# A decoder layer's expert stage: routing of two batches traced beside the items, weights in twelve buffers, products for counts five steps behind the choice, three experts with a first small item

## The chip, the cores and the metric

The kernel runs on one core of a Trainium2 chip. A core has five engines with a queue of instructions each, and a queue is worked through in order: TensorE (PE; its weight loads are shown apart as PEld), VectorE (DVE), ScalarE (ACT), GpSimd (POOL) and SyncE (SP), which here only issues DMAs. The metric is the device time of one execution in microseconds (us). Three executions of the kernel before gave 679.78, 682.89 and 682.9 us, with a median of 682.89 us.

## What is computed

One decoder layer on x of shape (4, 512, 256), in float32, three sublayers with a LayerNorm after each residual sum:

```python
x = layernorm(x + mamba(x))                    # scan over 512 steps, 16 states
x = layernorm(x + mlstm(q=x, k=ctx, v=ctx))    # 4 heads, causal, gated
# mixture of experts: 2048 tokens, 8 experts, the best two for each token
logits = x @ gate_w
mult, sel = sparse_mixer_top2(logits)
h = silu(einsum('th,ehf->etf', x, w1)) * einsum('th,ehf->etf', x, w3)
out = einsum('etf,efh,te->th', h, w2, w)       # w: mult at the chosen experts
x = layernorm(x + out)
```

An expert's weights are w1 and w3 (256 x 1024 each) and w2 (1024 x 256), 1 MB each. The kernel multiplies only the tokens that chose an expert.

## The kernel before

The first sublayer takes the trace up to about 165 us and is not touched. The rest is `layers23`.

**Attention** (`attend_fast`) goes over eight pairs of batch and half of the heads. In iteration n it makes the scores of pair n and the values of pair n-1, in four parts `tb`; the sums of the pair before that are gathered at the start (`gathered`, `gather`). When both pairs of a batch are gathered, a generator `finish(b)` is put into `tails`: this is the batch's **routing tail**. It holds the head norm (`den`, `vr`), logits and the first choice (`route`), the residual rows `hv`, then `close`: the statistics of the second LayerNorm (`norm_stats`), the normed rows `x`, which SP stores to DRAM (`xd`, up to three copies, and `yd`), and the rest of `route`. In `route`, two choices per token give `hot`; five small matrix products of `hot` (line 1717, the products for counts) give each token's position in its expert's list; DVE makes one-hot tiles `olo` and `oval`; eight products of those (line 1754) make `by`, the list of tokens by slot; `tables` turns it into the int32 tables for the gathers; a softmax (`ex`, `wk`) gives the multipliers, which are transposed (line 1792) and stored to DRAM (`wd`). The generator stops at each `yield`; `step()` runs the next piece of the oldest tail. In the kernel before, every part `tb` calls `step()` twice, so that the tails of batches 0, 1 and 2 are traced between parts of attention. Each tail has two square roots and one exponential on ACT.

**Experts.** An item is one block (128 tokens of an expert; "small item") or two blocks (256). `work` takes a list of items in order: `turn` (gathered rows are transposed, line 1277, DVE copies them), `up` (products with w1 and w3, line 1292; ACT takes Silu, line 1297; DVE multiplies, line 1298; one piece for each `yield`), then `down` of the item before (products with w2, line 1316; ACT weighs, line 1336; POOL adds the rows into `yd` by an indirect DMA, line 1322). Rows are gathered by POOL, two items ahead (`fetch`, line 1248). `early` holds one small item of each of the first NEARLY experts, with tokens of batches 0 and 1 only; `mid` a two-block item of each expert above NEARLY, with tokens of the first three batches, and another of expert 7; `late` all that is left but one expert, and five items whose expert is known only at run time; that one expert, number NEARLY, is taken by `finale` as four small items. With NEARLY at 2 there are 12 two-block items and 13 small ones, 37 blocks.

**Weights.** `load_expert` issues three DMAs of 1 MB on SP (w1, w3, w2) into one of three sets of tiles in turn. Two sets are loaded ahead of attention. The third set lies where attention keeps `x1T` and `val`, and can be filled only after these are done with. When the first item of an expert has been traced, the load of the expert two further on is traced. A `w1` tile becomes free when the former expert's `up` has ended, a `w2` tile when its `down` has.

**Order.** What is traced first has priority, but a planner orders each engine's queue when the program is built: from its own estimates of times it takes the first traced instruction that it holds to be ready. `keep_in_program_order` ties an instruction behind the one traced just before it on the same engine. In the layout of the pools, `np_` has one buffer for each name, `rt` two, the PSUM pool `pu` of `up` three banks, and `pt` (transposes and sums of heads) two.

At the end of `layers23` the kernel before does this, where `tails` then holds batch 3's tail alone:

```python
*done, last = tails
weights, pending = xp.work(xp.early, weights, xp.mid)
for _ in last:
    pass
weights, pending = xp.work(xp.mid + xp.late, weights, [xp.final], overflow_at_item_1, pending)
return xp.finale(xp.final, weights[0], pending)
```

So batch 3's tail is traced as one piece between the early items and the middle ones.

Of the kernel before, what the change touches and what calls it, by code (L numbers as in the profile page):

```python
# [27 lines left out]
NEARLY = 2  # L28
# [15 lines left out]
def decoder_kernel(ctx: ExitStack, tc: tile.TileContext, t: dict, out: bass.AP):  # L44
# [14 lines left out]
    def norm_stats(sp, src, n, tag):  # L59

        st = sp.tile([P, n, 6], F32, tag=tag + "st", name=tag + "st")
        mv = sp.tile([P, n, 2], F32, tag=tag + "mv", name=tag + "mv")
        for i in range(n):
            nc.vector.bn_stats(out=st[:, i, :], in_=src[:, i, :])
            nc.vector.bn_aggr(out=mv[:, i, :], in_=st[:, i, :])
        sd = sp.tile([P, n], F32, tag=tag + "sd", name=tag + "sd")
        nc.scalar.activation(sd, mv[:, :, 1], AF.Sqrt, bias=eps5)
        rs = sp.tile([P, n], F32, tag=tag + "rs", name=tag + "rs")
        nc.vector.reciprocal(rs, sd)
        return mv, rs  # L70
# [931 lines left out]
    def attend_fast(ap, hrp, np_, pt, tri, onw, mix, part, gatew, close, rt, route):  # L1002
# [4 lines left out]
        with ExitStack() as hs:  # L1007
# [170 lines left out]
            for n in range(len(pairs) + 1):  # L1178
# [6 lines left out]
                for tb in range(NB):  # L1185
# [13 lines left out]
                    step()  # L1199
                    step()  # L1200
# [14 lines left out]
    def experts(o, fast):  # L1215
# [5 lines left out]
        def load_expert(e):  # L1221

            nonlocal loads
            ew = o.ring[loads % 3]
            loads += 1
            w1 = ew.tile([P, 2, FF], F32, tag="w1", name="w1")
            w3 = ew.tile([P, 2, FF], F32, tag="w3", name="w3")
            w2 = ew.tile([P, NF, D], F32, tag="w2", name="w2")
            for w, n in ((w1, "w1"), (w3, "w3"), (w2, "w2")):
                nc.sync.dma_start(  # L1230
                    out=w, in_=t[n][bass.ds(e, 1)].rearrange("o (k p) f -> p (o k) f", p=P)
                )
            return w1, w3, w2
# [50 lines left out]
        def up(xT_, G, w1, w3, ht):  # L1284

            N, U = G * P, TS // (G * P)
            for f in range(0, NF, U):
                ps = o.pup.tile([P, 2, U, N], F32, tag="pu", name="pu")
                for u in range(U):
                    for j, w in enumerate((w1, w3)):  # L1290
                        for k in range(2):
                            nc.tensor.matmul(  # L1292
                                ps[:, j, u, :], w[:, k, (f + u) * P : (f + u + 1) * P],
                                xT_[:, k, :N], start=(k == 0), stop=(k == 1),
                            )
# [18 lines left out]
        def product(ps, g, G, ht, w2):  # L1314
            for f in range(NF):
                nc.tensor.matmul(  # L1316
                    ps, ht[:, (f * G + g) * P : (f * G + g + 1) * P], w2[:, f, :],
                    start=(f == 0), stop=(f == NF - 1),
                )
# [19 lines left out]
        def work(visits, weights, ahead=(), between=None, pending=None):  # L1339
# [6 lines left out]
            for i, (n, v, cols) in enumerate(line):  # L1346
# [4 lines left out]
                for _ in up(xT_, G, w1, w3, ht):  # L1351
                    pass
# [199 lines left out]
    def layers23(fast):  # L1552
# [4 lines left out]
        with ExitStack() as rest:  # L1557
# [125 lines left out]
            def route(b, base):  # L1683
# [32 lines left out]
                for i in range(5):  # L1716
                    nc.tensor.matmul(
                        pc, one_b if i else tri_b, hot[:, 4 - i : 9 - i, :],
                        start=(i == 0), stop=(i == 4),
# [29 lines left out]
                for j in range(NK):  # L1749
# [4 lines left out]
                    nc.tensor.matmul(  # L1754
                        pk, olo[:, j, :], oval[:, j, :], start=(j == 0), stop=(j == NK - 1)
# [36 lines left out]
                nc.tensor.transpose(bank[:NK, 384:], wk, ident)  # L1792
# [7 lines left out]
            def close(b, hv, routing=None):  # L1800
# [5 lines left out]
                mv, rs = norm_stats(np_, hv, NB, "n2")  # L1806
                yield
                next(routing)
# [10 lines left out]
                for rows in (*xds[max(b - 1, 0) :], yd):  # L1819
                    nc.sync.dma_start(  # L1820
                        out=rows[b * S : (b + 1) * S, :].rearrange("(i p) d -> p i d", p=P), in_=xb
                    )
                yield
# [102 lines left out]
            if tails:  # L1926
                *done, last = tails
                for tail in done:
                    for _ in tail:
                        pass  # L1930
            else:
                last = iter(())
            weights, pending = xp.work(xp.early, weights, xp.mid)
            for _ in last:
# [3 lines left out]
                pending,  # L1938
# [121 lines left out]
```

## Time and profile before

| What | Value |
|---|---|
| Median of three executions | 682.89 us |
| Profiled execution, its own time | 681.57 us |
| Span of its trace | 679.7 us |
| TensorE busy in the span | 645.8 us (95%) |
| VectorE, ScalarE, GpSimd busy | 307.8, 241.1, 209.0 us |
| Moved by DMA | 92.89 MB, mean 137 GB/s |
| Granted TensorE clock, mean | 0.978 |
| Weight DMAs | 57 of 1 MB |

Each line of the page's groups, or of a timeline, gives the engine, the line of the kernel, the operation, the tile written and those read with their shapes, and how many instructions are merged; a bracket at the end is idle time of that engine just before, and what ended it. float32 products appear as two records each, so a small item has 64 records of line 1292 and 16 of line 1316. A clock of 0.50 means that TensorE was granted half of its speed.

### The profile page before, as it was taken

How to read it: one execution, taken by the hardware profiler on the slowest of the kernel's cores; microseconds unless marked ns; L12 is line 12 of the kernel's file. 1: busy time of each engine (PE TensorE's matmuls, PEld its weight loads, DVE VectorE, ACT ScalarE, POOL GpSimd, SP SyncE). 2: the span in 40 equal slices, each digit the busy share in tenths (PEclk: the TensorE clock that was granted, in tenths of full speed). 3: DMA queues.
4: the chain of work that ended last, by engine and by line, in shares of the span. 5: the costliest groups of instructions: out<-in, count | busy, mean ns of one | idle time of the engine just before them, and what ended most of it. 6: DMA issues, size and time to landing. Idle time of an engine off the chain costs nothing. (4 is left out here: it accounts for less than half of the span.)

```text
span 679.7 us, 9237 instructions
## 1 busy us (share of the span) xinstructions
PE 645.8 (95%) x3447; PEld 497.9 (73%) x3447; DVE 307.8 (45%) x799; ACT 241.1 (35%) x473; POOL 209.0 (31%) x244
## 2 busy tenths in 40 slices
PE   6999999999997987899999999999999999999994
PEld 2434577766353447788888888888888899999993
DVE  1969658797557899662222221111211121121641
ACT  3965472132775754541121221112111111111452
POOL 0033400000564572743423244322432323423202
PEclk9999999999997996999999999999999999999998
DMA  8300501004603066856755335644463524883531
GB/s 279 121 1 0 186 1 32 31 1 160 242 1 124 9 196 216 285 170 209 220 169 179 86 94 154 194 153 137 150 209 78 152 78 148 272 316 86 176 113 36
DMA packets 61671, 92.89 MB, mean 137 GB/s; under 512 B 8904, under 2 KB 48784, under 8 KB 61360
## 3 DMA queue, kind: packets, MB, share of 16 engines
q1 hardware_dynamic: 52432, 80.51, 34.7%
q0 software_dynamic: 8096, 9.60, 7.2%
q10 hardware_dynamic: 1088, 2.10, 0.9%
q8 instruction: 29, 0.48, 0.3%
q14 instruction: 26, 0.21, 0.1%
HBM read 78.78 MB, written 14.06 MB: 137 GB/s over the span
## 5 line engine op out<-in xcount | busy, mean ns | idle before, releaser
L1292 PE MATMUL pu<-xgT,w 128*128 128x128 f32 (+1 forms) x1600 | 266.3, 327 | 1.0 <-DVE ht L1298 0.9
L1292 PEld LDWEIGHTS pu<-xgT,w 128*128 128x128 f32 x1600 | 243.0, 193 | 22.7 <-ACT x L1391 1.1
L1298 DVE TENSOR_TENSOR ht<-pu,si 128x256 f32<-128x256 f32 x148 | 62.6, 424 | 229.5 <-ACT si L1297 229.2
L1316 PE MATMUL po<-w,ht 128*128 128x256 f32 x592 | 136.7, 381 | 0.0
L1297 ACT ACTIVATE si<-pu 128x256 f32<-128x256 f32 x148 | 56.8, 384 | 195.6 <-PE pu L1292 195.3
L1316 PEld LDWEIGHTS po<-w,ht 128*128 128x128 f32 x592 | 109.8, 191 | 14.6 <-ACT y L1336 0.6
L1322 POOL DMA_INDIRECT yd<-y,tab x33 | 53.3, 1614 | 143.3 <-ACT y L1336 125.7
L232 PE MATMUL xz<-xT,win 128*128 128x512 f32 x128 | 58.3, 616 | 6.3 <-DMA xT<-in_xT 5.8
L1248 POOL DMA_INDIRECT xg<-xd,tab x37 | 36.8, 993 | 82.7 <-PE pt L1277 59.5
L232 PEld LDWEIGHTS xz<-xT,win 128*128 128x128 f32 x128 | 24.9, 198 | 38.8 <-issue 30.4
L1336 ACT ACTIVATE y<-po,wg 128x256 f32<-128x256 f32 x33 | 15.6, 474 | 93.8 <-PE po L1316 93.8
L1038 POOL TENSOR_TENSOR ct<-ct,tri 128x128 f32<-128x128 f32 x64 | 32.7, 530 | 34.0 <-ACT ct L1037 33.4
L460 PE MATMUL fpy<-mt,xs 128*128 128x384 f32 (+3 forms) x128 | 36.8, 438 | 0.5 <-DVE fsz L464 0.5
L255 DVE SCALAR_TENSOR_TENSOR acc<-xp,convw,acc 128x1024 f32<-128x1024 f32 x24 | 29.3, 1286 | 14.2 <-ACT acc L250 14.2
L1037 ACT ACTIVATE ct<-pq,eT 128x512 f32<-128x512 f32 (+3 forms) x64 | 29.9, 524 | 15.3 <-PE pq L1026 15.2
L1307 POOL DMA_INDIRECT wg<-wd,tab x33 | 31.9, 967 | 9.9 <-issue 9.6
L1026 PE MATMUL pq<-x1T,ctxT 64*128 64x512 f32 (+3 forms) x128 | 33.0, 486 | 1.6 <-ACT ct L1037 1.2
L1281 DVE COPY xgT<-pt 128x512 f32<-128x512 f32 (+1 forms) x22 | 12.5, 569 | 41.4 <-PE pt L1277 41.4
L460 PEld LDWEIGHTS fpy<-mt,xs 128*128 128x128 f32 x128 | 22.1, 190 | 12.3 <-issue 6.2
L485 PE MATMUL fpo<-fwout,fsz 128*128 128x256 f32 x128 | 28.9, 382 | 0.1
L485 PEld LDWEIGHTS fpo<-fwout,fsz 128*128 128x128 f32 x128 | 23.8, 190 | 4.7 <-issue 0.8
L1026 PEld LDWEIGHTS pq<-x1T,ctxT 64*128 64x128 f32 x128 | 13.7, 188 | 17.5 <-issue 8.0
(260 smaller groups left out, 612.9 us busy)
## 6 DMA issues: line engine op xcount, KB each, us to landing
w<-in_w SPq DMA_DIRECT2D x57, 1024.0 KB
xd<-x SPq DMA_DIRECT2D x9, 512.0 KB
xT<-in_xT ACTq DMA_DIRECT2D x4, 512.0 KB
ctxT<-in_ctxT SPq DMA_DIRECT2D x1, 2048.0 KB
val<-in_ctx SPq DMA_DIRECT2D x4, 512.0 KB
fxr<-in_x SPq DMA_DIRECT2D x4, 512.0 KB
yd<-x SPq DMA_DIRECT2D x4, 512.0 KB
x<-yd SPq DMA_DIRECT2D x4, 512.0 KB
```

What stands on the lines that cost most here:

```text
L232: nc.tensor.matmul(ps, win[:, k, c * P : (c + 1) * P], xT[:, k, b * S : (b + 1) * S], start=(k == 0), stop=(k == 1),)
L460: nc.tensor.matmul(ps[:, j * P :], xs[j][:, c, :], mt[b][j], start=(j == 0), stop=(j == NB - 1),)
L485: nc.tensor.matmul(ps, sz[:, c, b * S + i * P : b * S + (i + 1) * P], wout[:, c, :], start=(c == 0), stop=(c == NC - 1),)
L1026: nc.tensor.matmul(pss[e][:, cols[-1]], ctxT[rows, p, s0 : s0 + P], x1T[rows, p, s0 : (b + 1) * S], start=True, stop=True,)
L1038: nc.gpsimd.tensor_tensor(ct[:, :P], ct[:, :P], tri, ALU.mult)
L1248: nc.gpsimd.indirect_dma_start(out=xg[:, g, :], out_offset=None, in_=xds[min(v, 2)][:, :], in_offset=bass.IndirectOffsetOnAxis(ap=tok[v][: ...
L1292: nc.tensor.matmul(ps[:, j, u, :], w[:, k, (f + u) * P : (f + u + 1) * P], xT_[:, k, :N], start=(k == 0), stop=(k == 1),)
L1297: nc.scalar.activation(si, ps[:, 0].rearrange("p u n -> p (u n)"), AF.Silu)
L1298: nc.vector.tensor_tensor(ht[:, f * N : (f + U) * N], ps[:, 1].rearrange("p u n -> p (u n)"), si, ALU.mult)
L1307: issue = nc.gpsimd.indirect_dma_start(out=wg, out_offset=None, in_=wds[min(v, 2)][:, :], in_offset=bass.IndirectOffsetOnAxis(ap=wat[v][:, ...
L1316: nc.tensor.matmul(ps, ht[:, (f * G + g) * P : (f * G + g + 1) * P], w2[:, f, :], start=(f == 0), stop=(f == NF - 1),)
L1322: return nc.gpsimd.indirect_dma_start(out=rows[:, :], out_offset=bass.IndirectOffsetOnAxis(ap=dest[v][:, c : c + 1], axis=0), in_=src, in_ ...
```

## The change

Five edits, in the order of the file.

1. NEARLY goes from 2 to 3. `early` has three small items (experts 0, 1, 2), `mid` four two-block items (experts 4 to 7) and expert 7's second; `finale` takes expert 3. There are 11 two-block items and 15 small ones, still 37 blocks and 19 loads of an expert.
2. In attention, `step()` is no longer called in the last two iterations (n = 7 and 8). Batch 2's tail is left in `tails`, beside batch 3's.
3. `work` takes a generator `beside` and draws from it once after each piece of `up`. The early items get batch 2's tail, two steps a draw; the middle items get batch 3's tail, two steps a draw.
4. A tail has three more steps between the choice and the products for counts. These, the products for the list, the transpose of the multipliers, and the `bn_stats` of the second LayerNorm are tied behind what is traced just before them.
5. Weights are loaded in twelve pieces of 256 KB, each in a tile of its own: four of w1, four of w3, four of w2. A piece of w1 or w3 has 256 columns, so that a row in DRAM is cut into runs of 1 KB instead of 4 KB. The products read the piece that they need.

```diff
--- before.py
+++ after.py
@@ -1,4 +1,5 @@
 from contextlib import ExitStack
+from itertools import chain, zip_longest
 from types import SimpleNamespace
 
 import numpy as np
@@ -25,7 +26,7 @@
 NE, FF = 8, 1024
 NTT = NT // P
 TS = 256
-NEARLY = 2
+NEARLY = 3
 NOV = 31
 NOV0 = 5
 HCLIP = 100.0
@@ -56,12 +57,14 @@
         nc.sync.dma_start(out=c, in_=src)
         return c
 
-    def norm_stats(sp, src, n, tag):
+    def norm_stats(sp, src, n, tag, keep=False):
 
         st = sp.tile([P, n, 6], F32, tag=tag + "st", name=tag + "st")
         mv = sp.tile([P, n, 2], F32, tag=tag + "mv", name=tag + "mv")
         for i in range(n):
-            nc.vector.bn_stats(out=st[:, i, :], in_=src[:, i, :])
+            bn = nc.vector.bn_stats(out=st[:, i, :], in_=src[:, i, :])
+            if keep:
+                tc.keep_in_program_order(bn)
             nc.vector.bn_aggr(out=mv[:, i, :], in_=st[:, i, :])
         sd = sp.tile([P, n], F32, tag=tag + "sd", name=tag + "sd")
         nc.scalar.activation(sd, mv[:, :, 1], AF.Sqrt, bias=eps5)
@@ -1196,8 +1199,9 @@
                         residual(n // NH)
                     if n:
                         values(*pairs[n - 1], tb, cts[tb], po)
-                    step()
-                    step()
+                    if n < len(pairs) - 1:
+                        step()
+                        step()
                 if n:
                     sums = (*pairs[n - 1], po, hraw, sq2)
                 cts = nxt
@@ -1223,12 +1227,26 @@
             nonlocal loads
             ew = o.ring[loads % 3]
             loads += 1
-            w1 = ew.tile([P, 2, FF], F32, tag="w1", name="w1")
-            w3 = ew.tile([P, 2, FF], F32, tag="w3", name="w3")
-            w2 = ew.tile([P, NF, D], F32, tag="w2", name="w2")
-            for w, n in ((w1, "w1"), (w3, "w3"), (w2, "w2")):
+            w1, w3 = (
+                [ew.tile([P, 2, 2 * P], F32, tag=f"{n}{q}", name=n) for q in range(NF // 2)]
+                for n in ("w1", "w3")
+            )
+            w2 = [ew.tile([P, 2, D], F32, tag=f"w2{q}", name="w2") for q in range(NF // 2)]
+
+            for q in range(NF // 2):
+                for w, n in ((w1, "w1"), (w3, "w3")):
+                    nc.sync.dma_start(
+                        out=w[q],
+                        in_=t[n][bass.ds(e, 1), :, 2 * P * q : 2 * P * (q + 1)].rearrange(
+                            "o (k p) f -> p (o k) f", p=P
+                        ),
+                    )
+            for q in range(NF // 2):
                 nc.sync.dma_start(
-                    out=w, in_=t[n][bass.ds(e, 1)].rearrange("o (k p) f -> p (o k) f", p=P)
+                    out=w2[q],
+                    in_=t["w2"][bass.ds(e, 1), 2 * P * q : 2 * P * (q + 1), :].rearrange(
+                        "o (k p) f -> p (o k) f", p=P
+                    ),
                 )
             return w1, w3, w2
 
@@ -1287,10 +1305,11 @@
             for f in range(0, NF, U):
                 ps = o.pup.tile([P, 2, U, N], F32, tag="pu", name="pu")
                 for u in range(U):
+                    cols = slice((f + u) % 2 * P, ((f + u) % 2 + 1) * P)
                     for j, w in enumerate((w1, w3)):
                         for k in range(2):
                             nc.tensor.matmul(
-                                ps[:, j, u, :], w[:, k, (f + u) * P : (f + u + 1) * P],
+                                ps[:, j, u, :], w[(f + u) // 2][:, k, cols],
                                 xT_[:, k, :N], start=(k == 0), stop=(k == 1),
                             )
                 si = o.sip.tile([P, U * N], F32, tag="si", name="si")
@@ -1314,7 +1333,7 @@
         def product(ps, g, G, ht, w2):
             for f in range(NF):
                 nc.tensor.matmul(
-                    ps, ht[:, (f * G + g) * P : (f * G + g + 1) * P], w2[:, f, :],
+                    ps, ht[:, (f * G + g) * P : (f * G + g + 1) * P], w2[f // 2][:, f % 2, :],
                     start=(f == 0), stop=(f == NF - 1),
                 )
 
@@ -1336,7 +1355,7 @@
                 nc.scalar.activation(y[:, g, :], ps[:, g, :], AF.Copy, scale=wg[:, g : g + 1])
                 scatter(yd, v, c, y[:, g, :], compute_op=ALU.add)
 
-        def work(visits, weights, ahead=(), between=None, pending=None):
+        def work(visits, weights, ahead=(), between=None, pending=None, beside=iter(())):
 
 
 
@@ -1349,7 +1368,7 @@
                 w1, w3, w2 = weights[n]
                 ht = inner(G)
                 for _ in up(xT_, G, w1, w3, ht):
-                    pass
+                    next(beside, None)
                 if i + 2 < len(line):
                     xgs.append(fetch(*line[i + 2][1:]))
                 if pending is not None:
@@ -1714,9 +1733,11 @@
                 yield
                 pc = bank[:, 32 : 32 + 5 * NE].rearrange("p (n e) -> p n e", e=NE)
                 for i in range(5):
-                    nc.tensor.matmul(
-                        pc, one_b if i else tri_b, hot[:, 4 - i : 9 - i, :],
-                        start=(i == 0), stop=(i == 4),
+                    tc.keep_in_program_order(
+                        nc.tensor.matmul(
+                            pc, one_b if i else tri_b, hot[:, 4 - i : 9 - i, :],
+                            start=(i == 0), stop=(i == 4),
+                        )
                     )
                 yield
                 NK = 2 * NB
@@ -1751,8 +1772,10 @@
                         oval[:, j, :], i128, hi[:, j : j + 1],
                         vv[:, b * NK + j : b * NK + j + 1], ALU.is_equal, ALU.mult,
                     )
-                    nc.tensor.matmul(
-                        pk, olo[:, j, :], oval[:, j, :], start=(j == 0), stop=(j == NK - 1)
+                    tc.keep_in_program_order(
+                        nc.tensor.matmul(
+                            pk, olo[:, j, :], oval[:, j, :], start=(j == 0), stop=(j == NK - 1)
+                        )
                     )
                 nc.vector.tensor_tensor(count, pc[:, NB], count, ALU.add)
                 if 1 <= b < B - 1:
@@ -1789,7 +1812,7 @@
                 nc.vector.reciprocal(wk, su)
                 yield
 
-                nc.tensor.transpose(bank[:NK, 384:], wk, ident)
+                tc.keep_in_program_order(nc.tensor.transpose(bank[:NK, 384:], wk, ident))
                 wkT = rt("wkT", [NK, P])
                 nc.scalar.copy(wkT, bank[:NK, 384:])
                 for v in range(max(b - 1, 0), 3):
@@ -1803,9 +1826,8 @@
                 if routing is None:
                     routing = route(b, logits(b, hv))
                 next(routing)
-                mv, rs = norm_stats(np_, hv, NB, "n2")
+                mv, rs = norm_stats(np_, hv, NB, "n2", True)
                 yield
-                next(routing)
                 rstd[b] = rt("rstd", [P, NB])
                 nc.vector.tensor_copy(rstd[b], rs)
                 ms = np_.tile([P, NB], F32, tag="n2ms", name="n2ms")
@@ -1820,6 +1842,8 @@
                     nc.sync.dma_start(
                         out=rows[b * S : (b + 1) * S, :].rearrange("(i p) d -> p i d", p=P), in_=xb
                     )
+                yield
+                yield
                 yield
                 yield from routing
 
@@ -1923,19 +1947,16 @@
             o.htp, o.sip, o.yp, o.xtp, o.np3, o.fin, o.pup, o.pop, o.x1 = (
                 htp, sip, yp, xtp, np3, fin, pup, pop, x1
             )
-            if tails:
-                *done, last = tails
-                for tail in done:
-                    for _ in tail:
-                        pass
-            else:
-                last = iter(())
-            weights, pending = xp.work(xp.early, weights, xp.mid)
-            for _ in last:
+
+            *done, last = tails or [iter(())]
+            third = chain(*done)
+            third = zip_longest(third, third)
+            weights, pending = xp.work(xp.early, weights, xp.mid, beside=third)
+            for _ in third:
                 pass
             weights, pending = xp.work(
                 xp.mid + xp.late, weights, [xp.final], lambda i: overflow() if i == 1 else None,
-                pending,
+                pending, zip_longest(last, last),
             )
             return xp.finale(xp.final, weights[0], pending)
```

## The prediction

> **What bounds the kernel now.** I read the page's busy shares first (TensorE 95%), then busy time by stretch, since an average says nothing of where the other 5% lie.
>
> ```profile
> core 0: us, PE busy (x) PEld busy (x) DVE busy (x) ACT busy (x) POOL busy (x), PEclk, DMA share, GB/s
> 200.00:230.00 30.00, 25.81 (x122) 11.76 (x121) 22.19 (x78) 18.80 (x41) 15.62 (x26) 0.89 0.22 71
> 230.00:254.00 24.00, 21.75 (x124) 12.05 (x122) 22.65 (x77) 14.47 (x31) 16.71 (x28) 1.00 0.44 144
> 254.00:290.00 36.00, 28.12 (x191) 26.17 (x192) 28.19 (x124) 17.70 (x32) 18.65 (x21) 0.82 0.74 242
> 290.00:530.00 240.00, 240.00 (x1171) 211.38 (x1170) 55.75 (x153) 49.01 (x119) 79.55 (x68) 1.00 0.52 156
> 530.00:640.00 110.00, 110.00 (x753) 102.69 (x752) 23.07 (x64) 21.00 (x51) 35.24 (x29) 1.00 0.57 183
> ```
>
> From 290 to 640 us TensorE has no gap and its full clock: nothing gained on another engine, in the loads or in the routing shortens these 350 us. The change can gain only before 290, and there mostly from 254 to 290, where TensorE is idle for 7.9 of 36 us and slowed to 0.82 in the rest. The timeline of TensorE says why:
>
> ```profile
> 211.15 0.19 PE L1717 MATMUL prt<-hot,tri_b 128*128 128x40 bf16 x1 [2.49 <-DVE hot L1713]
> ...
> 252.27 1.51 PE L1046 MATMUL ph<-ct,val 128*64 128x384 f32 x10
> 257.43 2.29 PE L1060 MATMUL pth<-mix,hT 128*128 128x146 f32 x8 [3.65 <-DVE thr L1700]
> 260.65 0.19 PE L1717 MATMUL prt<-hot,tri_b 128*128 128x40 bf16 x1 [0.94 <-DVE hot L1713]
> ...
> 262.86 3.78 PE L1292 MATMUL pu<-xgT,w 128*128 128x128 f32 x16
> ...
> 281.46 3.19 PE L1316 MATMUL po<-w,ht 128*128 128x256 f32 x14
> 287.75 0.19 PE L1717 MATMUL prt<-hot,tri_b 128*128 128x40 bf16 x1 [3.10 <-DVE hot L1713]
> ```
>
> The last sums of heads (line 1060) wait for 3.65 us behind batch 2's routing on VectorE, and the products for counts (line 1717) wait for `hot` in three batches shown here. After such a gap the clock is halved: the 16 records at 262.86 take 3.78 us, where 64 of the same kind take 7.31 us later, so 1.83 us for 16.
>
> **What the stretch has lost.** From 253.78 (end of the values) to 290.50 (first `up` of `mid`) are 36.72 us. The work in it at full clock: 8 records of sums 1.26 (row at 251.08); batch 2's counts 0.33, list 1.95 (the 16 records at 292.78), transpose 0.11; a transpose for the range check 0.37; batch 3's counts 0.33; the first small item whole, 10.82; the second without its `down`, 7.37, and a quarter of that, 0.86; the turn of the next item 0.43. The 10.82 come from two starts of `up`:
>
> ```profile
> 590.34 7.31 PE L1292 MATMUL pu<-xgT,w 128*128 128x128 f32 x64
> 597.49 2.76 PE L1316 MATMUL po<-w,ht 128*128 128x256 f32 x12
> ...
> 601.16 1.05 PE L1292 MATMUL pu<-xgT,w 128*128 128x128 f32 x8
> ```
>
> Sum 23.83 us, so 12.89 us are lost to gaps and half clock. That is the most that the stretch can give.
>
> **Part by part.**
>
> *No steps in attention's last two iterations.* VectorE is busy for 22.65 of 24 us from 230 to 254 and is the engine that TensorE waits for at 257.43. Batch 2's instructions there now have lower priority than the last sums. TensorE then has work that waits for nothing of batch 2: early items need only the tables of batch 1 (rows gathered at 244.04 and 245.91) and weights landed by 181. Gone: the 3.65 and 0.94 us and the half clock behind them. What is late next is the copy of the sums (`hT`, 0.57 us at 253.96); I charge 1 us.
>
> *Batch 2's tail beside early items.* Two steps a draw, a draw for each quarter of `up` (7.31 / 4 = 1.8 us): its 16 steps end with the second item. The counts are step 10, after the first quarter of the second item, some 10.4 us after the first began; VectorE's work before them is about 11 us with the items' own (eight head-norm operations of 0.2, `lh` and `base` 0.85, two choices 2.0, `hv` 1.2, statistics 2.2, rest 0.7, items 2.5), and part of it can run before 254. Step 12, the list, comes one draw after the counts: between them stand six small operations of about 0.18, `olo` 1.21 and `oval` 2.4, in all 4.7 us against 1.8 us of TensorE. I charge 2 us, for later products of the items can go ahead. VectorE as a whole: about 16 us of tail and 6 of items in the 33 us until `mid` begins, so it isn't the bound.
>
> *Batch 3's tail beside the first middle item.* Its inputs are there by 262; its counts come five draws into an `up` of 13.98 us, near 299. Hidden behind 290 to 310, where VectorE is mostly free. The stop of 3.10 us should go. It was no slow product:
>
> ```profile
> 280.34 1.28 ACT L67 ACT_TABLE_LOAD   x1
> 286.30 0.30 ACT L67 ACTIVATE n2sd<-n2mv,eps 128x4 f32<-128x4 f32 x1 [4.68 <-DVE n2mv L65]
> 286.62 1.28 ACT L1297 ACT_TABLE_LOAD   x1
> 282.85 0.43 DVE L64 BATCH_NORM_STATS2 n2st<-hv 128x6 f32<-128x256 f32 x1 [4.20 <-POOL hv L1134]
> 282.09 2.79 POOL L1134 TENSOR_TENSOR hv<-hv,x 128x256 f32<-128x256 f32 x4
> ```
>
> GpSimd put nine indirect DMAs (270.42 to 282.07) ahead of `hv`; VectorE stood in the statistics for it, ScalarE in the square root for those, and behind that stood the Silu without which `down` can't go on. Tying `bn_stats` takes away VectorE's part of this. ScalarE's isn't tied, and now two tails, not one, stand beside Silus. One such stop costs 3.10 plus some 1.4 of half clock (four records at 288.80 take 1.92, not 0.86; the turn 1.10, not 0.60): 4.5 us. I charge 2 us, a chance near a half of one.
>
> [...] The rows show 1.28 us a load, a detour of 2 x 1.28 + 0.3 = 2.9 us, and TensorE can run ahead by the three banks of `pu`, each 1.8 us of work: 5.4 us. A detour whose input is ready is hidden; I take the row, so 0 for the loads and 2 us for late inputs.
>
> *Counts five steps behind the choice, in batches 0 and 1.* Now 2.49 us (batch 0) and 1.24 us (batch 1) of waiting, and about 2.4 us of half clock in the 4.9 us of products from 211 to 216: 6.1 us at most. VectorE is busy at 94% there, so part of the time is only moved: I take 3. Lower end 0; below nothing, it can delay batch 1's tables by three steps of some 1.4 us. The first early rows, gathered by 245.2, would then come at 249.4, still ahead of 254.5.
>
> *Three first small items.* One two-block item fewer (21.16 us, from 373.76 to 394.92), two small ones more (21.64): +0.48 us.
>
> *Weights in twelve pieces.* 57 issues become 228 at 0.37 us: SP holds 4.4 us per expert, and has nothing else to do there but the stores of `x`, which wait for ScalarE as before. Beyond earlier starts nothing is to be gained, for no product after 290 waits for a weight. A transfer of 1 KB runs costs more: the stores of `x`, which are such runs, moved 339 GB/s with all queues full (238 to 242); a load's first part, in 4 KB runs, 421 (564 to 568). An expert's 3.15 MB take 9.3 us at 339, against 10.8 us of a small item, the fastest turn; the first load of the dense end is issued 21 us ahead of its use (579.5 against 601.2). [...] The row decides; the charge is 0, at most 2 us for added waits in TensorE's queue.
>
> **Sum.** 681.57 - 12.89 - 3.0 + 0.48 + (1 + 2 + 2) = 671.2 us. The profiled execution is 1.3 under the median shown; half of that on top gives **672**. Its own range: charges of 1 and attention 5 give 665; three stops of ScalarE (13.5) and nothing in attention give 682.7, so 665 to 683.
>
> **Rivals.** *ScalarE's queue takes the gain back* (slower). Six detours stand beside items instead of three, planned by estimates that already failed once in this trace. At 4.5 us a stop, break-even lies at 12.89 / 4.5, near three; five stops give 681.57 - 12.89 + 0.48 + 22.5 = 691.7. For it: one of three did stop for 3.1 us. Against: the statistics are tied, TensorE's 5.4 us of slack, half of the tails' inputs ready early.
>
> *The first middle item comes late* (no change). Its rows need batch 2's whole tail and the stored `x`: in this trace 25 us from `den` (245.45) to the gather (270.42). From 255 that gives 280, and TensorE is due there at 253.78 + 33.4 = 287; if sharing VectorE and GpSimd with items stretches the tail by 15 us, 8 us of the gain go: 680.
>
> *The pieces don't do what they say:* without them, the weights of the first middle item would still have some 20 us, so the same 672; this can't be told by time alone.
>
> **Chances.** Forecast (666 to 679) 0.66, further gain below 666 0.04, first middle item late (679 to 686) 0.14, ScalarE 0.16. A change below 0.5%, 3.4 us, can't be told from none here. Faster 0.70, same 0.14, slower 0.16. Range 664 to 685.
>
> **What would show it.** Right: no gap over 1.5 us between 254 and 290, line 1060 without its 3.65 us, clock at 1.00 from 254 on, first product of `mid` near 290 with three small items done; after it TensorE still without gaps, and DMA share higher at equal bytes. Wrong: ScalarE rows with table loads followed by waits over 4 us beside Silus, or a gap in TensorE at a first product that reads a piece of weight.

## The result and the profile after

The kernel after took **688.16 us** (median of eight executions, 685.91 to 690.23) against 682.66 for the kernel before (also eight): ratio 1.0083, 95% interval 1.0061 to 1.0105. It is slower by 0.8%; 672 was forecast, with 0.16 for slower. The profiled execution took 687.57 us.

One thing must be known to read the numbers: one and the same kernel after gave 688 us in two sessions (a session: kernels run one after the other on one chip) and 677 us in a third, with every execution of a session on one side, and the traces tell the two apart. In one kind the trace has a semaphore record for every signal that the four compute engines send (1902 records for 1894 signalling instructions, in `e8` below); in the other dozens are missing (1825 for the same 1894). I call them *whole records* and *lost records*. Only semaphore records are lost, those of landed DMAs among them (5384 for 6584); rows of instructions are as many in both (9795). The result above fell on lost records; the trace of before, from which the forecast was made, has whole ones (1812 for 1804).

Busy time by stretch of the kernel after, the rows that answer to those of before:

```profile
230.00:254.00 24.00, 20.33 (x111) 10.37 (x112) 22.01 (x76) 14.70 (x30) 16.00 (x27) 1.00 0.36 116
254.00:290.00 36.00, 32.56 (x241) 29.58 (x241) 27.74 (x119) 18.93 (x31) 14.53 (x17) 0.95 0.81 252
290.00:530.00 240.00, 235.96 (x1152) 206.21 (x1152) 54.58 (x153) 50.18 (x119) 81.12 (x71) 0.98 0.56 156
```

From 254 to 290 TensorE is busy for 32.56 us, not 28.12, as meant. But after 290, where before had 240.00 of 240, 4 us are idle and the clock is 0.98. The first `up` of `mid` starts at 305.81. Before started it at 290.50 with one small item (10.82 us) less done, so at equal work at 301.32: the change is 4.5 us behind there, 0.48 more for the item it splits and about 1 in `finale` (TensorE's stop there is 1.96 us, 0.90 before) make the 6.0 between the profiled executions.

The timeline of all engines from 280 to 306, rows of three engines:

```profile
282.11 1.03 POOL L1266 DMA_INDIRECT xg<-xd,tab  x1 [1.17 <-issue]
...
284.19 4.69 PE L1311 MATMUL pu<-xgT,w 128*128 128x128 f32 x40
...
285.09 0.30 ACT L70 ACTIVATE n2sd<-n2mv,eps 128x4 f32<-128x4 f32 x1
...
290.64 0.73 PE L1311 MATMUL pu<-xgT,w 128*128 128x128 f32 x5 [0.43 <-issue]
...
290.75 1.28 ACT L1316 ACT_TABLE_LOAD   x1 [5.36 <-remote]
...
296.47 0.38 ACT L1316 ACTIVATE si<-pu 128x256 f32<-128x256 f32 x1 [3.56 <-remote]
...
297.96 0.94 POOL L1326 DMA_INDIRECT wgf<-wd,tab  x1 [0.30 <-issue]
...
299.91 4.42 PE L1335 MATMUL po<-w,ht 128*128 128x256 f32 x10 [0.88 <-issue]
...
300.81 0.38 ACT L1316 ACTIVATE si<-pu 128x256 f32<-128x256 f32 x1 [2.49 <-remote]
...
305.81 0.45 PE L1311 MATMUL pu<-xgT,w 128*128 128x256 f32 x1
```

This is the third small item. Its first quarter of `up`, 16 of the 40 records that take 4.69 us, ends near 286.1, its second near 288, its third at 291.37. ScalarE finishes its root at 285.39 and should begin the Silu's table once the first quarter is done. It begins at 290.75, the second Silu at 296.47, the third at 300.81, so 4.6, 8.5 and 9.4 us behind TensorE's rows: "remote" says that the awaited semaphore moved just then, with no instruction ending near it that could have moved it. TensorE fills its three banks of `pu` and then has to wait; 13.4 us pass for an `up` of 7.3, and the next products run at half clock (0.50 from 299.9 to 304.4: 10 records in 4.42 us, where 12 take 2.75 in `e8`). Its rows break up even before the third bank is full: its last eight records take from 289.25 to 291.37, with stops of 0.3 to 0.4 us for which the profile shows no cause ("issue"). All the while GpSimd issues indirect DMAs without a break, 13 of them from 282.11 to 298.90; the last late Silu comes through 1.9 us after that.

It looks like the rival *ScalarE's queue takes the gain back*: a table load, then a wait over 4 us. But ScalarE had finished its root at 285.39 and had only the Silu's table left to load. What came late is TensorE's result, as the others see it. (Whether the signal or the product behind it was late can't be told, as ends of TensorE's rows are modelled.)

### The profile page after: what moved, and what is told of

Read it like the earlier page. It is cut to its first block, busy times and chain, and to the rows that moved or that the text cites. A ratio compares the mean times of both kernels' runs of the same rounds, so it can differ in the third digit from the quotient of the medians.

```text
span 685.8 us, 9795 instructions
## 1 busy us (share of the span) xinstructions
PE 649.7 (95%) x3511; PEld 500.3 (73%) x3511; DVE 310.8 (45%) x800; ACT 244.1 (36%) x476; POOL 217.1 (32%) x244
## 5 line engine op out<-in xcount | busy, mean ns | idle before, releaser
L1311 PE MATMUL pu<-xgT,w 128*128 128x128 f32 (+1 forms) x1664 | 269.8, 322 | 5.6 <-issue 3.5
L1311 PEld LDWEIGHTS pu<-xgT,w 128*128 128x128 f32 x1664 | 246.1, 193 | 27.1 <-issue 5.6
L1335 PE MATMUL po<-w,ht 128*128 128x256 f32 x592 | 139.3, 385 | 1.1 <-issue 1.1
L1029 PE MATMUL pq<-x1T,ctxT 64*128 64x256 f32 (+3 forms) x128 | 32.3, 497 | 0.5 <-DVE lh L1113 0.3
L1299 DVE COPY xgT<-pt 128x256 f32<-128x256 f32 (+1 forms) x23 | 12.6, 550 | 38.8 <-PE pt L1295 38.6
L1049 PE MATMUL ph<-ct,val 128*64 128x512 f32 (+3 forms) x128 | 25.8, 470 | 1.6 <-POOL ct L1041 1.6
```

The costliest lines, as they stand in the source:

```text
L1029: nc.tensor.matmul(pss[e][:, cols[-1]], ctxT[rows, p, s0 : s0 + P], x1T[rows, p, s0 : (b + 1) * S], start=True, stop=True,)
L1311: nc.tensor.matmul(ps[:, j, u, :], w[(f + u) // 2][:, k, cols], xT_[:, k, :N], start=(k == 0), stop=(k == 1),)
L1335: nc.tensor.matmul(ps, ht[:, (f * G + g) * P : (f * G + g + 1) * P], w2[f // 2][:, f % 2, :], start=(f == 0), stop=(f == NF - 1),)
```

## The experiments

**1. Is it the pieces?** The three kernels here and the one under 2 ran in one session, and all had lost records. Whole weights, `e1_whole`, with loads and products to match:

```diff
-            w1, w3 = ([ew.tile([P, 2, 2 * P], F32, tag=f"{n}{q}", name=n) for q in range(NF // 2)] for n in ("w1", "w3"))
-            w2 = [ew.tile([P, 2, D], F32, tag=f"w2{q}", name="w2") for q in range(NF // 2)]
+            w1 = ew.tile([P, 2, FF], F32, tag="w1", name="w1")
+            w3 = ew.tile([P, 2, FF], F32, tag="w3", name="w3")
+            w2 = ew.tile([P, NF, D], F32, tag="w2", name="w2")
```

> The changed kernel, but with each expert's weights in three tiles of 1 MB again. In the changed kernel's trace the third early item takes 20.6 us (284.19 to 304.82) where a small item needs about 10.8, at a time when SP issues pieces of weights without a break. Theory W (the pieces' transfers hold up the engines there): that loss of 10 us goes, 677 to 680. Theory R (the routing tails beside the items hold up ScalarE and TensorE): the weights are innocent, 687 to 690. Theory E (a third early item is there too soon for its weights, which lie where attention kept its data): 688 or more, since a whole w1 lands later than its first piece.

The kernel before with the twelve pieces alone, `e2_pieces` (the same diff turned round, on before):

> The kernel before with the twelve pieces alone. Theory W: slower than before or the same, 683 to 688, and gaps of TensorE without a named releaser at the first items. Theories R and E: no difference, 681 to 684.

Eight pieces in runs of 4 KB, `e3_runs4k`:

```diff
-                [ew.tile([P, 2, 2 * P], F32, tag=f"{n}{q}", name=n) for q in range(NF // 2)]
+                [ew.tile([P, FF], F32, tag=f"{n}{k}", name=n) for k in range(2)]
```

> The changed kernel with w1 and w3 cut by halves of the contraction instead of by columns: 8 pieces per expert, runs of 4 KB as before. Theory W in the form that the many short runs do the harm: like the run with whole weights, 677 to 681. In the form that many DMAs do it: between, 682 to 686. Theories R and E: 687 to 690.

Measured: 689.22 (1.0088, 1.006 to 1.0116), 684.86 (1.0039, 1.0017 to 1.006) and 688.72 (1.0088, 1.0054 to 1.0122). With whole tiles the third item is held in the same way (its `up` starts at 283.62, `mid` at 304.33), so neither the pieces nor their 1 KB runs are the cause. Alone on before they cost 0.4%, in stops of 0.2 to 0.9 us beside GpSimd's row of gathers; 684.86 lies where theory W put it, just outside the 681 to 684 of the others.

**2. Is it the third item?** `e4_early2` sets `NEARLY = 2`.

> The changed kernel with NEARLY at 2: two small items first, as before; batch 2's tail still beside them. Theory E: 677 to 681, as no item then needs the third set of weights before the middle ones. Theory W: as the changed kernel, 686 to 690, with the loss moved to the first middle item. Theory R: 686 to 690, or worse, since the tail has fewer items to lie beside.

Measured 683.11 (1.0002, 0.9977 to 1.0026), which no theory had. `mid` now starts at 284.26, 6.2 us before that of the kernel before: the early items run as forecast. Then the first *middle* item is held, between 293 and 303 (stops of 2.57 and 4.50 us), and the gain is gone. So it isn't an item that stalls but a time, 285 to 303, in which GpSimd's row lies.

**3. Is it the row?** The one edit of `e5_pin_wg` and, on before, of `e6_before_pin_wg`:

```diff
-            if v == 0:
-                tc.keep_in_program_order(issue)
+            tc.keep_in_program_order(issue)
```

> The kernel after, with one condition less: all gathers of token weights (line 1326) keep their place in the program, where before only those of the first table did. GpSimd's unbroken row of 14 indirect DMAs from 282 to 299 us then splits: eight gathers of rows and one scatter at most stand together, the seven small ones (five wg, two wgf) come later, beside middle items. Theory R (TensorE's signals to ScalarE and VectorE arrive 4 to 9 us late for as long as GpSimd issues indirect DMAs without a break while the load queues are full): the third early item's up ends about 5 us sooner, time 682 to 685. Theory D (the full load queues alone do it) and theory T (ScalarE's detours to other tables do it): the gathers' order does not matter, 688 as before.

> The kernel before with the same one edit: gathers of token weights keep their place in the program. In the kernel before, three wg gathers stood ahead of hv on GpSimd (278.63 to 282.07), and hv's lateness ended in TensorE's stop of 3.10 us at 287.75. If GpSimd's queue is what made hv late, hv starts 3.7 us sooner, the stop of 3.10 us and the half clock behind it go, and the time is 678 to 680. If hv is late for another reason, 682 to 683. No theory expects it slower than 684. It is also the control for the trace: if signals are lost and late here too, the chip and not the change does it.

> The kernel after with two early items instead of three, whole weights (three tiles, 1 MB loads) and all gathers of token weights in program order: what stays of the change is the routing of the last two batches beside items and the later counts. With two early items alone the time was 683.1, with the first middle item held up from 289 to 306 us beside the same row of indirect DMAs. Theory R: with that row split and the weights' packets 4 KB, the hold-up is at most half of the 9 us seen there, and the kernel is the fastest so far, 675 to 679. Theories D and T: 682 to 684 as with two early items alone.

Measured 677.87 (0.9949, 0.9923 to 0.9974), 678.20 (0.9966, 0.9939 to 0.9992) and 673.75 (0.9875, 0.9821 to 0.9929). The first and the last are faster than even theory R had them. That looked like proof of theory R, and was not: the three ran on another chip, and their traces had whole records. (The row has 13 DMAs in the trace, not the 14 of the expectation.)

What `e6` does show is a gain of the kernel before's own. Its timeline from 277 to 288:

```profile
277.54 0.94 POOL L1307 DMA_INDIRECT wg<-wd,tab  x1 [0.30 <-issue]
278.50 2.80 POOL L1134 TENSOR_TENSOR hv<-hv,x 128x256 f32<-128x256 f32 x4
...
286.24 1.96 PE L1292 MATMUL pu<-xgT,w 128*128 128x256 f32 x8 [0.43 <-ACT x L1814]
```

One `wg` stands ahead of `hv` instead of three, `hv` starts at 278.50 instead of 282.09, and `mid` at 286.24 instead of 290.50 (of both differences 1.1 us are older, as the last sums come at 256.32 for 257.43): the stop of 3.10 us at the counts is 0.61. The prediction had this chain right.

**4. The control.** On one chip: the kernel after unchanged (`e8_after_again`), pinned (`e9_pin_wg_again`), two early items with whole weights without the pin (`e10_early2_whole`).

> The kernel after, unchanged, on the chip that also runs the next three. The first four experiments ran on one chip and showed late signals of TensorE and lost signal records; the pinned kernels ran on another and showed neither. Theory R (the unbroken row of 14 indirect DMAs holds the signals up): 688, ratio 1.008, with the third early item held up between 284 and 306 us as in the first trace. Theory C (the chip that ran it does it, and the pin gained little): on a chip that loses no records the kernel after is near 678, ratio 0.995.

> The kernel after with its gathers of token weights in program order, a second time, on the same chip as the kernel after. Theory R: 676 to 680 wherever it runs, 8 to 11 us under the kernel after. Theory C: equal to the kernel after beside it within 2 us, and on a chip that loses records it shows the late signals too.

> Two early items and whole weights, without the pin on the gathers of token weights: against the pinned 673.75 (ratio 0.9875) it gives the pin alone, against two early items in pieces (ratio 1.0002) the pieces alone. Theory R: the first middle item is held up beside the row of indirect DMAs, ratio 0.996 to 1.001. Theory C: ratio 0.987 to 0.990 as with the pin.

Measured 676.82 (0.992, 0.9887 to 0.9954), 678.29 (0.9938, 0.9917 to 0.9959) and 672.70 (0.985, 0.9806 to 0.9895), all with whole records. **The kernel after, unchanged, is here 0.8% faster than before**, and the pin is worth nothing. The same stretch in the timeline of `e8` (279 to 300):

```profile
279.97 1.03 POOL L1266 DMA_INDIRECT xg<-xd,tab  x1 [1.16 <-issue]
...
282.06 7.37 PE L1311 MATMUL pu<-xgT,w 128*128 128x128 f32 x64
...
284.14 1.28 ACT L1316 ACT_TABLE_LOAD   x1 [0.89 <-PE pu L1311]
...
286.21 0.37 ACT L1316 ACTIVATE si<-pu 128x256 f32<-128x256 f32 x1
...
287.95 0.37 ACT L1316 ACTIVATE si<-pu 128x256 f32<-128x256 f32 x1
...
293.28 6.93 PE L1311 MATMUL pu<-xgT,w 128*128 128x256 f32 x31
...
295.83 0.95 POOL L1326 DMA_INDIRECT wgf<-wd,tab  x1 [0.31 <-issue]
```

The same kernel, the same row of gathers (279.97 to 296.78 and on), the same detours of ScalarE between the Silus; but `up` takes 7.37 us, each Silu follows its quarter, and `mid` starts at 293.28. So the row of indirect DMAs by itself held up nothing here.

**5. Chip, or its state?** The kernel after (`e12_after_third`), before (`e13_before_again`) and `e10` (`e14_early2_whole_again`) once more, in one session.

> The kernel after, unchanged, a third time. So far 688.2 (ratio 1.0083) where the trace lost signal records and TensorE's signals came late, and 676.8 (ratio 0.992) where neither was seen. Theory C (the two times belong to the chip or its state at the time, and go with the lost records): either 687 to 690 with lost records and a third early item held up to 305 us, or 675 to 679 with no lost records and the first middle item at 293 us; nothing between, and no records lost in the second case. Theory L (each load of the program falls into one of the two by chance): the pairing with lost records may fail, or kernels of this call fall on different sides.

> The kernel before, unchanged, as a control on the same chip: its time beside itself gives the ratio 1.000 within 0.3% in any theory. Its trace tells what theory C leaves open: on a chip where the kernel after loses records, either the kernel before loses them too (then the loss belongs to the chip, and the kernel before has nothing that waits for the late signals), or it loses none (then the loss needs the changed kernel as well).

> Two early items and whole weights, without a pin, on the same chip as the two above. Where no records are lost it gave 672.7 (ratio 0.985), so 672 to 674 again. On a chip that loses them, theory C expects the first middle item held up from about 289 us as in the version in pieces with two early items (ratio 1.0002): 680 to 684. If it holds 673 there, whole loads are the cure, and the pieces are what the chip's state hurts.

Measured 687.85 (1.0062, 1.0041 to 1.0084), 681.19 (0.9982, 0.9949 to 1.0015) and 682.97 (1.0001, 0.9976 to 1.0027), all with lost records, on the chip that a quarter of an hour earlier gave 676.8 and 672.7 with whole ones. So it is not the chip as such, but a condition that lasted through each session. The kernel before loses records in it too (1739 for 1804) and hardly changes: TensorE is held for small stops near 281 (0.44 and 0.81 us), and its stop at the counts shrinks from 3.10 to 0.74. My reading, which no run tests: it had idle time where the hold falls, and the kernel after has filled it.

**6. The row again, with lost records.** `e15_early2_whole_pin_again` is `e7`, `e14` is the same without the pin.

> Two early items, whole weights, gathers of token weights in program order, a second time; the first run had whole signal records and gave ratio 0.9875. The same kernel without the pin gave 0.985 with whole records and 1.0001 with lost ones. If records are whole again: 0.985 to 0.989, and nothing new. If records are lost: theory R (late signals go with GpSimd's unbroken row of indirect DMAs, 16 long without the pin, 11 to 12 with it) expects the hold-up of the first middle item a third shorter or more, ratio 0.989 to 0.995; if the row's length does not matter, ratio 0.998 to 1.003 as without the pin.

It fell on lost records (1758 for 1810), on a third chip: 679.17, ratio 0.9932 (0.9901 to 0.9962) against 1.0001 (0.9976 to 1.0027) without the pin. The end of the row and what follows, without the pin (timeline from 292 to 306):

```profile
293.14 0.25 PE L1722 MATMUL prt<-hot,one_b 128*128 128x40 bf16 x4
...
298.28 0.94 POOL L1311 DMA_INDIRECT wgf<-wd,tab  x1 [0.30 <-issue]
301.44 0.94 ACT L1301 ACTIVATE si<-pu 128x256 f32<-128x256 f32 x3 [5.18 <-remote]
301.51 0.19 DVE L1733 TENSOR_TENSOR posm<-prt,count 128x32 f32<-128x32 f32 x1 [4.79 <-remote]
```

And with it (288 to 304):

```profile
293.54 0.25 PE L1721 MATMUL prt<-hot,one_b 128*128 128x40 bf16 x4
294.01 0.95 POOL L1311 DMA_INDIRECT wg<-wd,tab  x1 [0.30 <-issue]
...
296.84 1.00 ACT L1301 ACTIVATE si<-pu 128x256 f32<-128x256 f32 x3 [1.92 <-remote]
...
297.60 0.18 DVE L1732 TENSOR_TENSOR posm<-prt,count 128x32 f32<-128x32 f32 x1
```

Without the pin the row ends at 299.22, and three Silus held back come in one stroke at 301.44; VectorE reads at 301.51 counts that TensorE's row gives as done at 293.4. With the pin the row ends at 294.96, the Silus come at 296.84. From the row's last DMA to the release are 2.2 and 1.9 us. The other traces with lost records have it too: 298.90 to 300.81 in the first trace, 297.66 to 299.62 in `e12`, 298.35 to 299.52 in `e1`, 296.81 to 298.73 in `e3`, 299.42 to 301.69 in `e4`; and where the row ends some 15 us sooner, so does the hold: 284.27 to 285.88 in `e2`, 280.96 to 282.19 in `e13`. Nine traces agree on when the hold ends, so theory R fits, under lost records alone. The gain in time from a shorter row rests on one pair of runs, from two sessions on two chips, and whether the load queues must be full, as the theory has it, wasn't tested.

**7. A shorter row.** `e16_pin_rows_too` pins the gathers of rows as well, on two early items and whole weights; `e17` and `e18` repeat the pin on the kernel after, in the hope of lost records.

```diff
-                nc.gpsimd.indirect_dma_start(out=xg[:, g, :], ...)
+                issue = nc.gpsimd.indirect_dma_start(out=xg[:, g, :], ...)
+                tc.keep_in_program_order(issue)
```

> Two early items, whole weights, and now the gathers of rows (line 1266 of the kernel after) in program order as well as those of token weights. By the order of issue on GpSimd the row beside the first middle item falls from 12 indirect DMAs to seven (six gathers of rows and one of weights), then a scatter that waits for ScalarE. With lost records theory R expects the late signals to end some 5 us sooner than with the first pin alone (ratio 0.9932): 0.985 to 0.990. With whole records there is nothing to gain, and later gathers can only cost: 0.985 to 0.992. If the length of the row does not matter: 0.9932 or worse with lost records.

> The kernel after with its gathers of token weights in program order, a third time. With whole records it was 0.9949 and 0.9938. With lost records the kernel after itself is 1.006 to 1.008 with a row of 14; pinned, the row is nine (281 to 293 us in its trace with whole records). Theory R expects the release of the signals near 295 in place of 300.8, so 5 us less: 680 to 684, ratio 0.998 to 1.002. If the row's length does not matter: 1.006 to 1.009.

All had whole records. `e16` took 694.62 (1.0211, 1.0186 to 1.0236), outside every expectation. TensorE's timeline:

```profile
261.54 0.66 PE L1282 MATMUL pt<-ident,xg 128*128 128x128 f32 x2 [5.92 <-DVE n2mv L68]
...
294.33 1.54 PE L1282 MATMUL pt<-ident,xg 128*128 128x128 f32 x6 [4.50 <-DMA xg<-xd,tab]
300.54 0.47 PE L1282 MATMUL pt<-ident,xg 128*128 128x128 f32 x1 [4.67 <-DMA xg<-xd,tab]
```

The rows of the two early items, issued at 244.04 and 245.91 in the kernel before, are now issued at 258.62 and 259.94, behind the last sums (the wait of 5.92 is put down to VectorE, but the rows could not be turned before they had come); the middle rows at 289.10, behind a scatter that waits for ScalarE. Gathers of rows must go ahead of their place; those of weights need not. `e17` and `e18` gave 677.89 (0.9955) and 678.07 (0.9954), as twice before. What the pin does to the kernel after itself under lost records stays open.

**8. The counts.** `e11_pin_counts_back` takes the products for counts back to two steps after the choice, on the pinned kernel, in the session of 4 (whole records):

```diff
                 yield
+                next(routing)
                 rstd[b] = rt("rstd", [P, NB])
...
                 yield
-                yield
-                yield
                 yield from routing
```

> The kernel after, pinned, with the products for counts back where the kernel before had them: two steps after the choice began, not five. The prediction charged the later counts with a gain of 3 us in attention; the first trace showed none (a wait of 4.24 us instead of 2.49 in batch 0). If the prediction's term holds, this is 3 us slower than the pinned kernel beside it; if the later counts only move the wait, it is the same within 1 us; if they help where tails run beside items, the loss shows between 260 and 310 us in place of attention.

Measured 686.92 (1.0071, 1.0042 to 1.01) beside 678.29: 8.6 us, three times what the forecast gave the later counts. In attention the waits for `hot` are 3.91 and 2.39 us against 3.90 and 1.12 in `e9`. The timeline from 246 to 268 shows the end of the values and the last sums:

```profile
256.27 1.51 PE L1049 MATMUL ph<-ct,val 128*64 128x384 f32 x10
...
257.06 2.76 POOL L1137 TENSOR_TENSOR hv<-hv,x 128x256 f32<-128x256 f32 x4
257.10 2.77 DVE L1123 TENSOR_TENSOR base<-base,part 128x32 f32<-128x32 f32 x1
...
262.40 1.74 PE L1063 MATMUL pth<-mix,hT 128*128 128x146 f32 x8 [4.62 <-ACT hT L1058]
...
266.94 1.44 PE L1311 MATMUL pu<-xgT,w 128*128 128x128 f32 x5 [1.13 <-DVE xgT L1299]
```

The first `up` starts at 266.94 instead of 257.96 in `e9`, in two parts. Some 3.4 us are lost in attention: from batch 0's counts to the end of the values are 48.1 us (209.67 to 257.78) against 43.4 (209.37 to 252.81), with eight records of the last sums, 1.26 us, done more. That is the size that the forecast gave the later counts. The rest is lost at the last sums. With fewer steps before the counts, batch 2's routing stands ahead of them again, as in the kernel before: ScalarE, which must copy `hT` for them, stands for 4.87 us before an operation of batch 2 that waits for `base` on VectorE, and the sums wait for 4.62 us. The later counts thus are part of what frees the last sums; the forecast put that gain down to the missing steps alone.

## Why the prediction was wrong

*The condition.* The forecast was a sum over one trace with whole records, and the range 664 to 685 had no term for the other. The step that failed in that run is the overlap in which the third item was to lie. The sum took this item at full clock (10.82 us, +0.48 in all) and charged 2 us for late inputs of ScalarE, because "TensorE can run ahead by the three banks of `pu`", 5.4 us. Under lost records ScalarE saw TensorE's quarters 4.6 to 9.4 us late, TensorE ran out of banks, and the third item took from 284.19 to 305.81, 21.6 us, where with whole ones it took 11.2 (282.06 to 293.28). The charge of 2 us for batch 2's tail beside the first two items held: in `e8` the longest stop there is 1.18 us. The 10.4 us between the two third items are most of the 12 between the two profiled executions (687.57 and 675.55); 1.6 are the first `up`, here in part at half clock (0.50 from 261 to 263; 9.04 us against 7.41). I had seen GpSimd's row, "nine indirect DMAs (270.42 to 282.07) ahead of `hv`", as a queue that makes `hv` late, and had not asked what else stands beside it once TensorE is kept busy there. Why TensorE's results come late under lost records stays open.

*With whole records* the direction was right and the size was not: 675.55 for the profiled execution, 671.2 forecast. Point by point, by that trace:

- **The stretch**: 12.89 us lost before, 5 charged, so 7.89 to gain. From the end of the values (254.13) to 293.28 are 39.2 us for 23.83 + 10.82 + 1.26 = 35.91 of work, as eight records of sums that before had done at 251.08 now come behind the values: 3.2 lost, 9.6 gained. Right and more, and no stop of ScalarE of 4.5 us came. The gap of 3.65 is gone; at the last sums one of 0.64 is left.
- **The counts in attention**: 3.0 forecast, a loss of 1.6 measured: the values end 0.35 us later, with those eight records (1.26) still to do. This is the term that failed (4.6 us). Batch 0's wait grew from 2.49 to 3.91, since TensorE comes to the counts at 205.91, not 208.66; five steps or two make no difference there (3.90 and 3.91 in `e9` and `e11`). Batch 1's fell from 1.24 to 1.13, and two waits for GpSimd's `ct` before the last values are new (0.87 and 0.75). As `e11` loses another 3.4 us in attention without the later counts, some other part of the change costs that and more there; which one wasn't taken apart.
- **The item split**: 0.48 stands; it wasn't measured by itself.
- **Not in the sum**: `finale` waits for 1.75 us instead of 0.90, and batch 3's counts (0.33) now lie behind the stretch. 4.6 less the 1.8 gained on the stretch beyond the forecast, and 0.85 and 0.33 more, make 4.0 of the 4.35 us; the rest is unexplained.
- **The third item** was taken as neutral but for 0.48. With lost records it costs 5 us (1.0083 to 1.0002). With whole ones, it and the pieces together cost 4 (676.8 to 672.7); which of the two wasn't taken apart.
- **The pieces**: 0 charged, at most 2. With two early items and lost records, pieces and whole weights are equal (1.0002 and 1.0001); on before they cost 0.4%. Right for the first, just over the bound for the second (2.3 us). The charge of 0 was an estimate from six loads of 1 MB that SP issued in a row: from 162 to 181 in the trace of before the DMA share is 0.97.
- **Rivals**: *ScalarE's queue* gave the sign and nearly the size (691.7) by the wrong mechanism: with whole records the same detours stand beside Silus, about 2.9 us each (in `e8` two loads of 1.28 us with 0.26 or 0.30 between them, from 281.67 and 288.33), and no stop of TensorE there is put down to ScalarE (the longest, 1.18 us, to VectorE's `wk`). *The first middle item comes late* happened in neither.

**A version faster than both**: two early items, whole weights, the rest of the change and the pin: 0.9875 with whole records, 0.9932 with lost ones. Without the pin it is 0.985, but 1.0001 with lost ones. That leaves the routing beside the items and the later counts as what pays; the ties of edit 4 were in all these versions and weren't tested alone.

## What to carry to other kernels

A kernel with idle time on the bound engine can hide a disturbance that the same kernel, once tightened, passes on to its end (so I read 681.19 us before and 687.85 after, both with lost records); ask of each wait that you remove what else it was covering. Before you explain a surprise by the change, run the same program again in another session: here the same code, run again, was 1.6% faster, and the theory built on the first trace fitted one condition only. And a gather that a planner may issue early is better tied to its place only if its data isn't needed there at once (`e6`, weights tied: 0.9966; `e16`, rows tied as well: 1.0211).

## What the hardware showed

- **Two conditions**, with lost and with whole signal records, that lasted through a session: 687.9 and 676.8 us for one kernel on one chip. Under lost records GpSimd's unbroken row of indirect DMAs goes with results of TensorE that others see late (4.6 to 9.4 us in the first trace), until 1.2 to 2.3 us after the row's end in nine traces. What sets the condition wasn't found. A rival that stays open is the recording itself: every execution timed here has a span and a granted clock from the profiler, so none shows what an unrecorded one takes. No run here tests it.
- **A VectorE operation took longer beside GpSimd's**: `base`, 128x32, took 2.77 us in `e11` beside the four instructions of `hv` on GpSimd and ended with the last (259.87 and 259.82). In the trace of before it took 0.19 us with no `hv` beside it (228.18) and 0.53 when it began 0.25 us into the first of the four, each of 0.7 (253.26). There it ended at 253.78, the first of the four at 253.74. That VectorE waits for GpSimd is my reading of these three rows; no run moves `hv` alone to test it.
